# Layer 2 keys: statistics a batch ahead, a second key buffer, half-row token layout, the bound of the scores a batch late

## The chip, the cores and the metric

The kernel runs on one core of one Trainium2 chip. The metric is the device time in microseconds (us) of one execution, start to end; the median of three timed runs before the change is 7727.34 us (7716.75 to 7728.98). Beside the timed runs there is one profiled execution, from which every trace number here is read.

## The reference

The reference is a four-layer network on an image batch `x` of shape (8, 56, 56, 128), float32. Layer 0 is a deformable convolution block, layer 1 whitens the result (64 rows, five Newton-Schulz steps), layers 2 and 3 are attention followed by a mixture of 64 experts. Only the attention of layer 2 matters here. Each image becomes S = 3136 tokens of 128 channels (56 x 56, row by row), and the attention works on normalised tokens:

```python
def _ln_t(v, eps=1e-5):
    m = jnp.mean(v, axis=-1, keepdims=True)
    s = jnp.var(v, axis=-1, keepdims=True)
    return (v - m) / jnp.sqrt(s + eps)

# layer 2 attention, HEADS = 8, D_K = 16
kqv = x @ W_k.T
h = kqv.reshape(B, S, HEADS, D_K).transpose(0, 2, 1, 3)
scores = jnp.einsum('bhqd,bhkd->bhqk', h, h) / jnp.sqrt(jnp.float32(D_K))
attn = jax.nn.softmax(scores, axis=-1)
ctx = jnp.einsum('bhqk,bhkd->bhqd', attn, h)

# how it is used
t = t + _L2_attn_ref(_ln_t(t), L2_attn_W_k, L2_attn_W_q, L2_attn_W_v, L2_attn_W_o)
```

Queries, keys and values are the same projection `h`. So the kernel needs, for each of the 8 images, the normalised tokens, the keys with channels on partitions (`kT`), the values with tokens on partitions (`va`), and one number for all images: a bound on the scores, from the largest squared length of a head's vector, which lets the softmax do without a maximum per row.

## The kernel before, in words

The kernel runs the layers one after the other: `conv_layer`, `whiten_layer` (which leaves its result `y` in device memory as [56 rows, 8 images, 56 columns, 128 channels]), and `token_layers`. The last begins with a few transposed weights, calls `attention_keys` once, and then `attend`, the long part of the kernel, which reads the keys and values back from device memory.

`attention_keys` loops over the 8 images ("batches", `n`). For one batch it does this, in the order of the program:

1. Load the tokens into `t_sb`, a tile of 112 partitions by 28 tokens by 128 channels (lines 1060 to 1062), in two transfers of 56 partitions: partition `h * 56 + w` holds the tokens of column `w` in the image rows of parity `h`. In device memory each run is one token, 512 bytes. Line 1063 stores the same tile to `tok`, the token list that the later stage reads, also 512 bytes a run. The tile `t` has two buffers.
2. Statistics, lines 1066 to 1068: 28 pairs of `bn_stats` and `bn_aggr` on VectorE (DVE).
3. `rsqrt` (lines 1136 to 1142): DVE adds the epsilon (line 1140), GpSimd (POOL) raises to the power -0.5 (line 1141). The result `rs` has 112 x 28 elements.
4. Seven groups of four token columns: DVE normalises each 112 x 128 piece (`normalize`, line 112) into `xn` (two buffers), TensorE (PE) transposes it (line 121), ScalarE (ACT) copies the group out of PSUM into a 448-wide piece of `xT` (line 122), the normalised tokens with channels on partitions. `xT` has two buffers.
5. Keys: for two groups of heads, seven matmuls of 448 columns (line 1083), moved out of PSUM alternately by DVE (line 1091, even) and ACT (line 1087, odd) into `kT`, which has one buffer. Each half is then stored (line 1094).
6. Values: 25 matmuls of up to 128 tokens (line 1098), moved out alternately by DVE (line 1108) and ACT (line 1106) into `va`, one of two standing buffers, then stored in two transfers (line 1110).
7. The bound: POOL squares all values (line 1117), DVE sums each head's 16 squares (line 1119, 128 x 3200 elements in) and takes the largest (line 1120) into column `n` of `tops`.

After the loop a short chain turns `tops` into `low` and the flag `small`, on which the branch to `attend` waits. All PSUM tiles of the stage share six buffers (tag `m`).

All token, key and value transfers are issued by SyncE (SP) on one queue, in order: an instruction of that queue that waits holds up those behind it. The order of the instructions on each engine is not that of the program. A planner runs through the program with costs of its own and lets each engine take the earliest instruction of the program that is ready by these costs; so work of the next batch can be placed into gaps of the present one, and a transfer ahead of others. The order is fixed when the kernel is built; on the chip each engine goes through its list and waits where an input is late. `advance` (line 438), used by the change, steps the first generator of a list to its next `yield` and drops it when it is done; it fixes only where in the program the instructions stand.

Of the kernel before, what the change touches and what calls it, by code (L numbers as in the profile page):

```python
# [8 lines left out]
F32 = mybir.dt.float32  # L9
# [3 lines left out]
ALU = mybir.AluOpType  # L13
AX = mybir.AxisListType
# [3 lines left out]
NB, IH, IW, C = 8, 56, 56, 128  # L18
S = IH * IW
T = 112  # L20
NT = S // T
GT = 4
NG = NT // GT
QC = GT * T
KT = -(-S // 128)
# [19 lines left out]
HD, DK = 8, 16  # L45
# [71 lines left out]
def transpose_group(nc, k, ps, tag, dst, src, copy):  # L117

    p = ps.tile([128, GT, T], F32, tag=tag, name="p_tr")
    for i in range(GT):  # L120
        nc.tensor.transpose(p[:, i, :], src[:, i, :], k.ident[:T, :T])  # L121
    copy(dst, p.rearrange("p a b -> p (a b)"))  # L122
# [315 lines left out]
def advance(gens, n=1):  # L438

    for g in list(gens[:n]):  # L440
        try:
            next(g)
        except StopIteration:
            gens.remove(g)
# [591 lines left out]
    return [(t, min(128, S - 128 * t)) for t in range(KT)]  # L1036


def attention_keys(tc, k, w, yv, tok, kT_out, va_out, low, small):

    nc = tc.nc
    n_b = yv.shape[1]
    with ExitStack() as ctx:
        cp = ctx.enter_context(tc.tile_pool(name="akc", bufs=1))
        bp = ctx.enter_context(tc.tile_pool(name="akb", bufs=2))
        ps = ctx.enter_context(tc.tile_pool(name="akp", bufs=6, space=PSUM))
        vas = []  # L1050
        for i in range(2):
            va = cp.tile([128, 2, KT, 4, 32], F32, name=f"va{i}")
            nc.gpsimd.memset(va, 0.0)
            nc.gpsimd.memset(va[:, :, : KT - 1, :, DK : DK + 1], 1.0)
            nc.gpsimd.memset(va[: S - 128 * (KT - 1), :, KT - 1, :, DK : DK + 1], 1.0)
            vas.append(va)
        tops = cp.tile([128, n_b], F32, name="tops")
        wk = w.wk.rearrange("p h d -> p (h d)")
        for n in range(n_b):
            t_sb = bp.tile([T, NT, C], F32, name="t")  # L1060
            for h in range(2):
                nc.sync.dma_start(t_sb[h * IW : (h + 1) * IW], yv[h, n])
            nc.sync.dma_start(tok[n].rearrange("(t p) c -> p t c", p=T), t_sb)
            mv = bp.tile([T, NT, 2], F32, name="mv")
            st = bp.tile([T, NT, 6], F32, name="st")
            for i in range(NT):
                nc.vector.bn_stats(st[:, i], t_sb[:, i])
                nc.vector.bn_aggr(mv[:, i], st[:, i])
            rs = rsqrt(nc, k, bp, mv, NT)
            xT = bp.tile([C, S], F32, name="xT")  # L1070
            for g in range(NG):
                xn = bp.tile([T, GT, C], F32, name="xn")
                for i in range(GT):
                    normalize(nc, xn[:, i], t_sb[:, g * GT + i], mv, rs, g * GT + i)
                transpose_group(
                    nc, k, ps, "m", xT[:, g * QC : (g + 1) * QC], xn, nc.scalar.copy
                )
            kT = bp.tile([128, 2, S], F32, name="kT", bufs=1)
            for g in range(2):
                for c in range(NG):  # L1080
                    cols = slice(c * QC, (c + 1) * QC)
                    p = ps.tile([128, QC], F32, tag="m", name="p_h")
                    nc.tensor.matmul(
                        p, wk[:, g * 128 : (g + 1) * 128], xT[:, cols], start=True, stop=True
                    )
                    if c % 2:
                        nc.scalar.activation(
                            kT[:, g, cols], p, AF.Identity, bias=w.one16, scale=DK**-0.25
                        )
                    else:  # L1090
                        nc.vector.tensor_scalar(
                            kT[:, g, cols], p, DK**-0.25, w.one16, ALU.mult, ALU.add
                        )
                nc.sync.dma_start(kT_out[n, g], kT[:, g])
            va = vas[n % 2]
            for t, m in key_tiles():
                p = ps.tile([128, 2, 4, DK], F32, tag="m", name="p_v")
                nc.tensor.matmul(
                    p[:m].rearrange("p g j d -> p (g j d)"),
                    xT[:, t * 128 : t * 128 + m],  # L1100
                    w.wv,
                    start=True,
                    stop=True,
                )
                if t % 2:
                    nc.scalar.copy(va[:m, :, t, :, :DK], p[:m])
                else:
                    nc.vector.tensor_copy(va[:m, :, t, :, :DK], p[:m])
            for g in range(2):
                nc.sync.dma_start(va_out[n, g], va[:, g].rearrange("p t j d -> p (t j d)"))  # L1110

            sq = bp.tile([128, 2 * KT * 4, DK], F32, name="sq", bufs=1)
            v = va.rearrange("p g t j d -> p (g t j) d")[:, :, :DK]
            nc.gpsimd.tensor_tensor(sq, v, v, ALU.mult)
            top = bp.tile([128, 2 * KT * 4], F32, name="top")
            nc.vector.tensor_reduce(top, sq, AX.X, ALU.add)
            nc.vector.tensor_reduce(tops[:, n : n + 1], top, AX.X, ALU.max)  # L1120

        col = cp.tile([128, 1], F32, name="top_c")
        nc.vector.tensor_reduce(col, tops, AX.X, ALU.max)
        p = ps.tile([1, 128], F32, tag="m", name="p_tc")
        nc.tensor.transpose(p, col, k.ident)
        one = cp.tile([1, 1], F32, name="top_1")
        nc.vector.tensor_reduce(one, p, AX.X, ALU.max)
        p = ps.tile([128, 1], F32, tag="m", name="p_low")
        nc.tensor.matmul(p, k.ones, one, start=True, stop=True)
        nc.vector.tensor_scalar(low, p, -(DK**-0.5), None, ALU.mult)  # L1130
        nc.vector.tensor_scalar(small, low[:1], -SMALL, None, ALU.is_ge)
        nc.vector.tensor_scalar(low, low, 1.0, None, ALU.subtract)
        nc.vector.tensor_tensor(low, low, w.one16, ALU.mult)


def rsqrt(nc, k, pool, mv, n):

    m = mv.shape[0]
    rs = pool.tile([m, n], F32, name="rs")
    nc.vector.tensor_scalar(rs, mv[:, :, 1], EPS, None, ALU.add)  # L1140
    nc.gpsimd.tensor_tensor(rs, rs, k.mhalf[:m, :n], ALU.pow)  # L1141
    return rs
# [1037 lines left out]
def token_layers(tc, k, a, y, out):  # L2180

    nc = tc.nc
    n_b = out.shape[0]
    with ExitStack() as ctx:
# [6 lines left out]
        kT_d = dp.tile([n_b, 2, 128, S], F32, name="kT_d")  # L2191
# [6 lines left out]
        with tc.tile_pool(name="tlr", bufs=1) as rp:  # L2198
# [33 lines left out]
            yv = y.rearrange("(t a) n w c -> a n w t c", a=2)  # L2232
            low = cp.tile([128, 1], F32, name="low")
            small = cp.tile([1, 1], I32, name="small")
            attention_keys(tc, k, w, yv, tok, kT_d, va_d, low, small)
        pooled = [cp.tile([C, n_b, E], F32, name=f"pooled{i}") for i in range(2)]
        low3 = cp.tile([128, 1], F32, name="low3")
        small3 = cp.tile([1, 1], I32, name="small3")
# [105 lines left out]
```

## Time and profile before

| what | value |
|---|---|
| median of three timed runs | 7727.34 us (7716.75, 7727.34, 7728.98) |
| the profiled execution: time and span | 7718.14 us, 7716.3 us |
| share of the span busy: PE, DVE, ACT, POOL | 84%, 68%, 54%, 38% |
| key stage: first token load issued, last values stored to `va` | 1589.5 us, 1933.0 us |
| DVE per batch: 28 normalisations; 28 statistics pairs; 8 key evictions; 13 value copies; the two reductions | 7.3; 7.3; 8 x 0.68; 13 x 0.29; 3.5 + 0.3 us |
| ACT per batch: 7 `xT` copies; 6 key evictions; 12 value copies | 7 x 0.53; 6 x 0.63; 12 x 0.27 us |
| POOL per batch: power; squares | 4.8; 5.5 us |
| bytes per batch: tokens in, tokens out, keys, values | 1.61, 1.61, 3.21, 3.28 MB |
| token packets: size | 512 bytes (51,378 of the stage's 55,491 packets are of 512 bytes to 2 KB) |

The stage takes about 344 us, 4% to 5% of the span. How to read the views: a line of the timeline has the start, the time taken, engine, source line, operation, output and inputs by their names in the program and the shapes; in square brackets the idle time in front of it and what ended that. Similar neighbours are merged. In the view of waits, "A <- B" is how long A's engine stood before A and was released by B: total, times, longest. In the groups, the numbers behind the bar are total busy time and the mean of one in nanoseconds. The stretches give each engine's busy time with the instruction count in brackets. PE's float32 matmuls run as two passes, each its own entry (an 'x28' of key matmuls in the trace is 14 in the program).

### The profile page before, as it was taken

Reading aid. Unit: us, or ns where it says so; the run is one execution under the profiler, and the core shown is the slowest. Engines: PE = TensorE matmul, PEld = TensorE weight load, DVE = VectorE, ACT = ScalarE, POOL = GpSimd, SP = SyncE. Lnnn points to the kernel's source line nnn. Section 1 sums busy time; section 2 is a strip of 40 time slices with the busy share of each in tenths; the row PEclk is TensorE's granted clock in tenths of the full one; section 3 lists DMA queues with packets and bytes.
Section 4 is the critical chain, followed back from the end, with each engine's and each line's share of the span. In section 5 each row is a group of like instructions: output and inputs, shape, how many; then the busy total and the mean of one; then the engine's idle time right before and its main releaser. Section 6 shows DMA issues by size and latency. Waiting matters only on the chain. (4 is left out here: it accounts for less than half of the span.)

```text
span 7716.3 us, 157926 instructions
## 1 busy us (share of the span) xinstructions
PE 6482.3 (84%) x59883; PEld 2880.7 (37%) x59883; DVE 5284.8 (68%) x9856; ACT 4142.6 (54%) x6467; POOL 2935.1 (38%) x2555
## 2 busy tenths in 40 slices
PE   6659999556899999999999999999999997556654
PEld 4446666334233323323323323333333333245532
DVE  7975564366677777777777777777777776366752
ACT  4424444122666666666666666666666664056740
POOL 0011111022444444444444444444444443434653
PEclk8768898777999999999999999999999998788766
DMA  5453443376788778778778778778778775543543
GB/s 155 137 119 76 86 95 65 82 240 207 199 203 197 193 192 199 189 192 201 191 184 204 188 183 207 183 191 205 185 190 206 182 190 137 196 117 107 134 135 130
DMA packets 736303, 1287.38 MB, mean 167 GB/s; under 512 B 117698, under 2 KB 503108, under 8 KB 728516
## 3 DMA queue, kind: packets, MB, share of 16 engines
q1 hardware_dynamic: 725556, 1260.76, 65.1%
q0 software_dynamic: 6144, 12.60, 0.6%
q8 instruction: 484, 7.93, 0.5%
q10 hardware_dynamic: 3824, 3.68, 0.2%
q14 instruction: 295, 2.42, 0.1%
HBM read 286.04 MB, written 197.81 MB: 63 GB/s over the span
## 5 line engine op out<-in xcount | busy, mean ns | idle before, releaser
L1260 ACT ACTIVATE e<-p_s 128x768 f32<-128x768 f32 (+2 forms) x3712 | 2887.8, 830 | 1584.9 <-PE p_s L1252 1329.8
L1298 POOL COPY x<-sq 32x1152 f32<-32x1152 f32 x1792 | 2059.2, 1149 | 2067.6 <-PE p_s L1252 1330.0
L1271 DVE STREAM_TRANSPOSE sq<-e 128x768 f32<-128x768 f32 x2688 | 2434.5, 950 | 567.3 <-ACT e L1260 312.9
L1252 PE MATMUL p_s<-q,kT 32*128 32x384 f32 (+2 forms) x14848 | 1888.6, 548 | 33.6 <-ACT e L1260 18.6
L1305 PE MATMUL av<-e,va 128*32 128x384 f32 (+2 forms) x14848 | 1645.3, 515 | 30.4 <-DVE acc L1324 20.7
L1305 PE MATMUL avx<-x,va 128*32 128x384 f32 x10752 | 1138.3, 496 | 69.5 <-issue 40.2
L1252 PEld LDWEIGHTS p_s<-q,kT 32*128 32x128 f32 (+1 forms) x14848 | 654.8, 181 | 1252.6 <-issue 825.4
L1305 PEld LDWEIGHTS av<-e,va 128*32 128x32 f32 (+1 forms) x14848 | 294.5, 108 | 1049.4 <-issue 941.7
L1305 PEld LDWEIGHTS avx<-x,va 128*32 128x32 f32 x10752 | 353.2, 111 | 650.9 <-issue 595.2
L609 POOL TENSOR_TENSOR rs<-rs,mhalf 112x4 f32<-112x4 f32 x112 | 116.1, 1036 | 788.3 <-DVE rs L608 788.3
L1324 DVE TENSOR_TENSOR acc<-acc,avx 128x384 f32<-128x384 f32 x336 | 183.9, 547 | 229.9 <-PE avx L1305 228.6
L121 PE MATMUL p_tr<-ident,xn 112*128 112x112 f32 x672 | 134.6, 341 | 187.4 <-DVE xn L112 141.8
L1141 POOL TENSOR_TENSOR rs<-rs,mhalf 112x4 f32<-112x4 f32 (+2 forms) x136 | 168.1, 1236 | 269.3 <-DVE ntop L1942 123.8
L525 ACT COPY wT<-p_w 88x448 f32<-88x448 f32 x152 | 138.0, 922 | 194.1 <-PE p_w L523 161.4
L1990 ACT ACTIVATE xn<-t,ms,rs 112x128 f32<-112x128 f32 x448 | 185.3, 488 | 76.4 <-DVE ms L1983 76.4
L327 DVE SCALAR_TENSOR_TENSOR acc<-xp,dw,acc 128x3136 f32<-128x3136 f32 x56 | 194.3, 3478 | 31.3 <-ACT acc L322 31.2
L637 PE MATMUL p_f<-x1T,w 128*128 128x448 f32 x448 | 205.6, 583 | 4.4 <-DVE x1T L632 2.7
L121 PEld LDWEIGHTS p_tr<-ident,xn 112*128 112x128 f32 x672 | 98.7, 169 | 285.0 <-issue 185.1
L1385 POOL TENSOR_TENSOR rs<-rs,mhalf 128x3 f32<-128x3 f32 (+1 forms) x72 | 58.5, 815 | 365.0 <-DVE rs L1384 343.0
L523 PE MATMUL p_w<-ident,wide 112*88 112x112 f32 x896 | 146.5, 303 | 58.6 <-DMA px<-strips 34.1
L621 DVE TENSOR_TENSOR y<-y,p_rs 128x448 f32<-128x448 f32 x112 | 69.3, 619 | 176.6 <-PE p_rs L614 176.6
L122 ACT COPY xT<-p_tr 128x448 f32<-128x448 f32 x112 | 59.6, 532 | 229.8 <-PE p_tr L121 203.7
(354 smaller groups left out, 7830.9 us busy)
## 6 DMA issues: line engine op xcount, KB each, us to landing
x<-sq SPq DMA_DIRECT2D x5376, 144.0 KB
w<-in_L_ffn_weight_dram SPq DMA_DIRECT2D x64, 1024.0 KB
px<-strips SPq DMA_DIRECT2D x64, 616.0 KB
va_d<-va SPq DMA_DIRECT2D x16, 1600.0 KB
xT_d<-xT SPq DMA_DIRECT2D x112, 224.0 KB
xT<-xT_d SPq DMA_DIRECT2D x112, 224.0 KB
kT_d<-kT SPq DMA_DIRECT2D x16, 1568.0 KB
t<-t_a SPq DMA_DIRECT2D x16, 1568.0 KB
```

What stands on the lines that cost most here:

```text
L121: nc.tensor.transpose(p[:, i, :], src[:, i, :], k.ident[:T, :T])
L327: nc.vector.scalar_tensor_tensor(acc, xp[:, j // 3 : j // 3 + IH, j % 3 : j % 3 + IW], dw[:, j : j + 1], acc, ALU.mult, ALU.add,)
L523: nc.tensor.transpose(p[:, g], around[:, :, g], k.ident[:T, :T])
L637: nc.tensor.matmul(p, q.w1[:, f * 128 : (f + 1) * 128], x1T, start=True, stop=True)
L1141: nc.gpsimd.tensor_tensor(rs, rs, k.mhalf[:m, :n], ALU.pow)
L1252: nc.tensor.matmul(ss[j // 2][:m, j % 2, :width], kT[rows, 128 * i : 128 * i + m], q[rows, :width], start=True, stop=True,)
L1260: nc.scalar.activation(e[:m, 2 * j : 2 * j + 2, :width], ss[j][:m, :, :width], AF.Exp)
L1271: nc.vector.transpose(sq[:, :, i, j : j + 2].rearrange("p s j c -> p j s c"), exps[u, b, a, i][:, j : j + 2, :QB].rearrange("p j (s c) -> ...
L1298: nc.gpsimd.tensor_copy(*moves.pop(0))
L1305: nc.tensor.matmul(out, keys[u, b][1][:m, i, j, :], e[j], start=start, stop=stop)
L1324: nc.vector.tensor_tensor(to, to, in_order(av), ALU.add)
L1990: nc.scalar.activation(out[:, i], x[:, i], AF.Identity, bias=ms[:, i : i + 1], scale=rs[:, i : i + 1])
```

## The change

The tokens are laid out differently: partition `f * 56 + h` now holds the 28 tokens of half `f` of image row `h`. A partition's tokens are one run of 14,336 bytes in `y` and in `tok`; load and store are two transfers of 56 partitions each. Since a transposed group of four now holds tokens that are 28 apart, PE's output is viewed as [channels, 4, 2, 56], and ACT's copy writes it to its places in `xT`, 56 elements in a row of steps of 56 elements (224 bytes); `xT` ends in token order as before, but each group writes columns all over it.

Loading, statistics and `rsqrt` become a generator, `statistics(n)`. That of batch 0 runs at the start. In batch `n` that of `n + 1` is started before the normalisation and stepped after each of the 14 key matmuls: the tokens' store and four statistics pairs in the first step, four pairs in each of the next six, `rsqrt` in the eighth. The bound becomes a generator, `largest(n)`: the squares stand where they stood, after batch `n`'s values, but the two reductions come after the normalisation of batch `n + 1`. `kT` gets the pool's two buffers. Arithmetic and the number of compute instructions are the same; there is one token store more per batch.

```diff
-        for n in range(n_b):
+        def statistics(n):
             t_sb = bp.tile([T, NT, C], F32, name="t")
-            for h in range(2):
-                nc.sync.dma_start(t_sb[h * IW : (h + 1) * IW], yv[h, n])
-            nc.sync.dma_start(tok[n].rearrange("(t p) c -> p t c", p=T), t_sb)
+            inner = tok[n].rearrange("(h f i) c -> f h i c", f=2, i=NT)
+            for f in range(2):
+                of = slice(f * IH, (f + 1) * IH)
+                nc.sync.dma_start(t_sb[of], y[:, n, f * NT : (f + 1) * NT])
+            yield
+            for f in range(2):
+                nc.sync.dma_start(inner[f], t_sb[f * IH : (f + 1) * IH])
             mv = bp.tile([T, NT, 2], F32, name="mv")
             st = bp.tile([T, NT, 6], F32, name="st")
             for i in range(NT):
                 nc.vector.bn_stats(st[:, i], t_sb[:, i])
                 nc.vector.bn_aggr(mv[:, i], st[:, i])
-            rs = rsqrt(nc, k, bp, mv, NT)
+                if i % GT == GT - 1:
+                    yield
+            stats[n] = t_sb, mv, rsqrt(nc, k, bp, mv, NT)
+
+        def largest(n):
+            sq = bp.tile([128, 2 * KT * 4, DK], F32, name="sq", bufs=1)
+            v = vas[n % 2].rearrange("p g t j d -> p (g t j) d")[:, :, :DK]
+            nc.gpsimd.tensor_tensor(sq, v, v, ALU.mult)
+            yield
+            top = bp.tile([128, 2 * KT * 4], F32, name="top")
+            nc.vector.tensor_reduce(top, sq, AX.X, ALU.add)
+            nc.vector.tensor_reduce(tops[:, n : n + 1], top, AX.X, ALU.max)
+
+        stats, tail = {}, []
+        ahead = [statistics(0)]
+        while ahead:
+            advance(ahead)
+        for n in range(n_b):
+            t_sb, mv, rs = stats.pop(n)
+            if n + 1 < n_b:
+                ahead.append(statistics(n + 1))
+                advance(ahead)
             xT = bp.tile([C, S], F32, name="xT")
+            by_place = xT.rearrange("c (h f i) -> c i f h", f=2, i=NT)
             for g in range(NG):
...
-                transpose_group(
-                    nc, k, ps, "m", xT[:, g * QC : (g + 1) * QC], xn, nc.scalar.copy
-                )
-            kT = bp.tile([128, 2, S], F32, name="kT", bufs=1)
+                p = ps.tile([C, GT, 2, IH], F32, tag="m", name="p_tr")
+                for i in range(GT):
+                    nc.tensor.transpose(
+                        p[:, i].rearrange("c f h -> c (f h)"), xn[:, i], k.ident[:T, :T]
+                    )
+                nc.scalar.copy(by_place[:, g * GT : (g + 1) * GT], p)
+            advance(tail)
+            kT = bp.tile([128, 2, S], F32, name="kT")
             for g in range(2):
                 for c in range(NG):
...
                         p, wk[:, g * 128 : (g + 1) * 128], xT[:, cols], start=True, stop=True
                     )
+                    advance(ahead)
...
-            sq = bp.tile([128, 2 * KT * 4, DK], F32, name="sq", bufs=1)
-            v = va.rearrange("p g t j d -> p (g t j) d")[:, :, :DK]
-            nc.gpsimd.tensor_tensor(sq, v, v, ALU.mult)
-            top = bp.tile([128, 2 * KT * 4], F32, name="top")
-            nc.vector.tensor_reduce(top, sq, AX.X, ALU.add)
-            nc.vector.tensor_reduce(tops[:, n : n + 1], top, AX.X, ALU.max)
+            tail.append(largest(n))
+            advance(tail)
+        while tail:
+            advance(tail)
```

The caller passes `y` itself instead of its view by row parity.

More of the change, by code (lines that the diff above doesn't have):

```diff
@@ L1036, in key_tiles, with attention_keys @@
     return [(t, min(128, S - 128 * t)) for t in range(KT)]
-def attention_keys(tc, k, w, yv, tok, kT_out, va_out, low, small):
+def attention_keys(tc, k, w, y, tok, kT_out, va_out, low, small):
     nc = tc.nc
-    n_b = yv.shape[1]
+    n_b = y.shape[1]
     with ExitStack() as ctx:
@@ L1094, in attention_keys @@
                 nc.sync.dma_start(kT_out[n, g], kT[:, g])
+            assert not ahead
             va = vas[n % 2]
@@ L2234, in token_layers @@
             small = cp.tile([1, 1], I32, name="small")
[L2235 removed]
+            attention_keys(tc, k, w, y, tok, kT_d, va_d, low, small)
         pooled = [cp.tile([C, n_b, E], F32, name=f"pooled{i}") for i in range(2)]
```

## The prediction

> **What bounds the kernel now.** I read the page, then the stretches, the waits, the groups and the timeline of the one stage the change touches. The chain of work that ended last is no help: it covers the last 1% and lies in another stage. The key stage runs from the first token load (SP, 1589.5 us) to the last value tile (1933.0 us). One batch, by stretches (us, busy time of PE, weight loads, DVE, ACT, POOL, then granted clock, DMA share, GB/s):
>
> ```profile
> 1691.28:1734.60 43.32, 24.84 (x106) 16.56 (x106) 27.37 (x109) 10.72 (x25) 10.31 (x2) 0.70 0.71 225
> ```
>
> No engine fills it: PE works 24.8 of 43.3 us, DVE 27.4. So order of work sets the time, as that batch's timeline shows (start, us, what):
>
> ```profile
> 1681.66 3.49 DVE L1119 TENSOR_REDUCE top<-sq 128x200 f32<-128x3200 f32 x1 [2.75 <-POOL sq L1117]
> ...
> 1686.45 4.79 POOL L1141 TENSOR_TENSOR rs<-rs,mhalf 112x28 f32<-112x28 f32 x1 [4.82 <-DVE rs L1140]
> 1691.28 7.28 DVE L112 TENSOR_SCALAR xn<-t,mv,rs 112x128 f32<-112x128 f32 x28 [4.91 <-POOL rs L1141]
> ...
> 1691.78 6.58 PE L121 MATMUL p_tr<-ident,xn 112*128 112x112 f32 x25 [16.16 <-DVE xn L112]
> ...
> 1700.23 10.67 PE L1083 MATMUL p_h<-xT,wk 128*128 128x448 f32 x26
> ...
> 1710.73 5.88 PE L1098 MATMUL p_v<-wkT,xT 128*128 128x128 f32 x50
> ...
> 1717.10 5.52 POOL L1117 TENSOR_TENSOR sq<-va 128x3200 f32<-128x3200 f32 x1 [25.86 <-DVE va L1108]
> ```
>
> After one batch's values come the squares on POOL (5.5 us), their reduction on DVE (3.5), the last statistics, the power on POOL (4.8), and only then the next batch is normalised; PE stands still for 16.2 us. Over the stage (total us, times, longest):
>
> ```profile
> POOL sq L1117 <- DVE va L1108: 205.1, 8, 26.6
> ...
> PE p_tr L121 <- DVE xn L112: 141.8, 8, 28.6
> ...
> DVE xn L112 <- POOL rs L1141: 32.4, 8, 5.0
> ```
>
> The first normalisations, right after each power, begin at 1614.6, 1650.0, 1691.3, 1734.5, 1786.8, 1823.1, 1864.9 and 1908.3: a mean period of (1908.3-1614.6)/7 = 42.0 us. Most statistics of batch n+1 already lie between the evictions of batch n, so it is the tail (reduction, power) that is late, and in some batches the load: the 52.3 us period has tokens landing at 1774.3.
>
> **What the Trainium skill says.** (1) "SBUF — State Buffer", section "Who interferes with whom": a tensor_scalar in SBUF can take the port pair that DVE shares with GpSimd; the pair is an exclusive lock, and tensor_reduce never takes it. The trace agrees. The first line below is a 0.18 us instruction that stood behind the squares (POOL, 1639.51 to 1645.03); the second is four normalisations that at 0.26 us a step should take 1.1 us and took 2.1, behind a POOL addition (7435.47, 1.26 us):
>
> ```profile
> 1640.08 4.99 DVE L1140 TENSOR_SCALAR rs<-mv 112x28 f32<-112x28 f32 x1
> ...
> 7435.51 2.08 DVE L112 TENSOR_SCALAR chosen<-chosen,cmv,rs 128x128 f32<-128x128 f32 x4
> ```
>
> (2) "DMA: Bandwidth & Descriptors", "Specifications", gives 512 bytes as the least for line rate. The trace disagrees: with only 512-byte token runs in flight it moved 181 GB/s (1596 to 1602) and 168 (1650 to 1653) at full DMA share; rows of 12 KB of keys and values moved 410 (1641 to 1647) and 419 (1677 to 1686). The measurement decides. (3) The same page, "Why a DMA increments its semaphore by 16 and not by 1": a copy of 56 rows is spread over 14 engines (largest divisor up to 16). No run shows it; I take 14/16 of 410 = 359 GB/s. (4) "SBUF", "Specifications (TRN2)": leaving a 16-byte line at each element costs. It agrees with two copies of one shape, dense and strided (448 bytes a step), 532 against 926 ns:
>
> ```profile
> L122 ACT COPY xT<-p_tr 128x448 f32<-128x448 f32 x112 | 59.6, 532 | 229.8 <-PE p_tr L121 203.7 <-ACT xn L1990 17.6 <-issue 8.5
> ...
> L551 ACT COPY smp<-p_smp 128x448 f32<-128x448 f32 x56 | 51.9, 926 | 110.8 <-PE p_smp L544 110.4
> ```
>
> **The change, part by part.**
>
> *Half rows.* Loads and stores of tokens (1.61 MB each way a batch) go from 512 B to 14,336 B runs. At about 175 GB/s they take 18.4 us a batch, then 2 x 1.61/0.359 = 9.0. With 6.49 MB of keys and values at 0.41 (15.8 us) DMA needs 24.8 us a batch; before it was some 34 of 42. SP has the same four token, key and value issues plus one more store (0.4 us). The first load, issued at 1589.5, landed at 1601.9; now 4.5 us of transfer and about 2 us of latency (estimate: the time between the last bytes and later waits of this queue) give 1596. Gain 5.9 us. If 56 rows ran no faster than 512 B pieces, this is nothing.
>
> *Strided xT.* 56 copies grow from 532 to about 926 ns (steps of 224 bytes; the 112-byte copy on line 525 takes 922). A group of four normalisations takes 4 x 0.26 = 1.04 us, so ACT keeps pace and only the last group shows: +0.4 us a batch. But now every copy writes columns all over xT, so the first key matmul waits for the seventh copy: from the first normalisation 7.3 + 0.4 (PE) + 0.9 + 0.3 = 8.9 us, where it was 6.9. If a copy cost more than 1.04 us, each 0.1 us above adds 0.7 us a batch.
>
> *Statistics ahead.* The 28 pairs (28 x 0.26 = 7.3 us of DVE) and the power (4.8, POOL) move under batch n's key matmuls. The power leaves the path; POOL is idle there, so it costs nothing; without that cover it is 4.8 us a batch. Behind the statistics on DVE stand the key evictions, and behind those PE, which has six PSUM buffers of lead. The next tokens land in time: queued behind 3.28 MB of values they need 8.0 + 4.5 + 2 = 14.5 us from the batch's start, and DVE asks at 11 to 17.
>
> *Second kT.* The store of the old keys made others wait 0.6 us in all: nothing, either way.
>
> *Bound late.* The reduction (3.5 + 0.3) follows the next normalisation, so PE works beneath it. The squares still start when the values end, which is now when DVE wants to normalise. By (1) one blocks the other: a loss between 0 and 5.5 us a batch. I take 5.5, since DVE either stands in the normalisation or, if it keeps the ports, then at the reduction that waits for the squares.
>
> *Sum.* A middle batch on DVE from its first normalisation: 7.3 + 5.5 stall + 3.8 reductions = 16.6; statistics 7.3 and the four DVE evictions of the first key half 4 x 0.68 = 2.7, so 26.6; PE was held by PSUM and does its last two key tiles, 1.5, so 28.1; 25 value tiles at 0.235 (5.88/25) = 5.9; last copy 0.3. Together 34.3 us. The first batch has no stall: 8.9 + 14 x 0.75 + 6.2 = 25.6, say 26. The last has no statistics: 12.8 + 1.6 + 10.5 + 6.2 = 31. The first normalisation moves from 1614.6 to 1608.7. End of values: 1608.7 + 26 + 6 x 34.3 + 31 = 1871.5 instead of 1933.0. Gain 61.5 us. What follows (last squares, bound, attention) does the same as before. The span of 7716.3 becomes 7654.8, the profiled run of 7718.1 becomes 7656.6. The timed runs were 7716.8, 7727.3 and 7729.0; with the profiled one their mean is 7722.8, and 7722.8 - 61.5 = 7661 is my number.
>
> **Rivals.**
>
> *A, 0.50:* as summed, 7661; its own range is 7645 to 7680.
>
> *B, 0.25: no stall.* The code is put in order by a planner that filled DVE gaps with other batches' work before; it may put statistics or some normalisations under the squares or before them. Then 7.3 + 3.8 + 10 + 1.5 + 5.9 + 0.3 = 28.8 a batch: 6 x 5.5 + 5.5 = 38.5 more, 7622. For it: bn_stats has one SBUF input and ran under the squares at 0.25 us. Against: rs was planned beneath the squares and stood.
>
> *C, 0.15: the order stays.* If the planner believes the tokens late, statistics fall behind the values again and the power stays on the path. Only the transfers gain: 5.9 at the start and about 3 us a period (a mean of 39, the undisturbed ones being 35.4 and 41.3), 7 x 3 + 5.9 = 27, 7696. For it: in batches 4 and 7 they fell there. Against: that was after late loads, now halved.
>
> *D, 0.05: slower, by the strided copy.* If the 224-byte step with 56 in a row costs far more than both strided copies measured, ACT sets the transposes' pace: the gain is gone when 56 x (c - 1.04) = 61.5, c = 2.1 us, and 0.2% is lost from 2.4 us. Both known strides stand at 0.92 to 0.93, so this is remote; at 2.6 us it gives 7748.
>
> The remaining 0.05 is no difference that can be told, by two small failures together.
>
> **How the numbers follow.** About 0.2%, 15 us, is what a measurement of this kernel can tell from no change. A, B and C are faster by more: 0.90; same 0.05; slower 0.05. The range takes in B's and C's times with a few us for the runs' spread: 7614 to 7698.
>
> **What would show it.** Right: powers begin during the key matmuls; PE's wait for xn falls from 141.8 to about 60 us; one normalisation or reduction of 4 to 5.5 us per batch beside the squares; xT copies near 0.92 us; token landings 6 to 7 us after an idle queue; periods near 34. Wrong: xT copies above 1.1 us; powers still after the squares; DVE waiting for t in every batch; tokens under 200 GB/s; or another stage changing by more than 10 us.

## The result, and the profile after

The change makes the kernel slower. The median is 7774.03 us (7767.39 to 7781.31, four runs) against 7725.65 (7716.75 to 7728.98) before: a ratio of 1.0065, 95% interval 1.0047 to 1.0082, where the prediction had 7661. The profiled spans are 7773.5 and 7716.3 us. The key stage carries nearly all of it: from the first normalisation to the last squares on POOL it took 1610.8 to 1978.0 = 367.2 us after, and 1614.6 to 1933.2 = 318.6 before: 48.6 us more. The spans differ by 57.2 us; 12.4 of these lie behind the stage, where the program is unchanged, and the first normalisation comes 3.8 us earlier.

The stretches of the changed kernel first, one batch from normalisation to normalisation (columns as in the prediction: PE, weight loads, DVE, ACT, POOL, then clock, DMA share, GB/s):

```profile
1699.50:1750.24 50.74, 26.78 (x106) 17.23 (x106) 27.70 (x108) 13.93 (x25) 10.32 (x2) 0.67 0.55 193
```

PE has the 106 matmuls and DVE the work that they had in the 43.3 us of before. PE is busy 1.9 us longer, at a lower clock (0.67 against 0.70), and ACT 3.2 us, by the strided copies; what grew most is the time in which PE stands still. The timeline of the next batch shows where:

```profile
1728.35 5.52 POOL L1087 TENSOR_TENSOR sq<-va 128x3200 f32<-128x3200 f32 x1 [28.87 <-DVE va L1147]
...
1733.90 3.49 DVE L1090 TENSOR_REDUCE top<-sq 128x200 f32<-128x3200 f32 x1 [5.72 <-POOL sq L1087]
1737.42 0.36 DVE L1091 TENSOR_REDUCE tops<-top 128x1 f32<-128x200 f32 x1
1737.70 0.48 DVE L1075 BATCH_NORM_STATS2 st<-t 112x6 f32<-112x128 f32 x2
...
1745.41 4.80 POOL L1174 TENSOR_TENSOR rs<-rs,mhalf 112x28 f32<-112x28 f32 x1 [11.54 <-DVE rs L1173]
1750.24 7.27 DVE L112 TENSOR_SCALAR xn<-t,mv,rs 112x128 f32<-112x128 f32 x28 [4.91 <-POOL rs L1174]
1750.73 7.28 PE L1110 MATMUL p_tr<-ident,xn 112*128 112x112 f32 x28 [22.87 <-DVE xn L112]
...
1759.08 12.32 PE L1120 MATMUL p_h<-xT,wk 128*128 128x448 f32 x28 [1.07 <-ACT xT L1113]
1771.24 5.88 PE L1137 MATMUL p_v<-wkT,xT 128*128 128x128 f32 x50
1777.61 5.52 POOL L1087 TENSOR_TENSOR sq<-va 128x3200 f32<-128x3200 f32 x1 [27.41 <-DVE va L1147]
```

The statistics, which the change says are a batch ahead, stand behind the values, the squares and the reductions. The pause from the squares' start to the next normalisation, 1750.24 - 1728.35 = 21.9 us, is a chain: squares 5.5, reductions 3.9, 28 statistics pairs 7.5, `rs` and power 5.1. None lies under PE, and in that order the late bound is not late either. Six of the seven pauses are of this length. Before, pauses varied from 10.5 to 27.6 us, since most statistics lay between evictions in some batches; seven together were 113.6 us, now 128.6 (the first counts as -2.6, since its normalisation begins before the squares). The rest of the 48.6 us is the way from normalisation to squares: 25.6 us on average before, now 34.8 in batches 0 and 1 (in the first the statistics fall inside it, in the second the normalisation begins among the values and stands beside the squares), and 27.4 to 28.9 after that. Of these last 2.6 us or so, 1.9 are the wait for all seven strided copies, which was forecast.

The waits of the stage (total us, times, longest) answer those of before:

```profile
POOL sq L1087 <- DVE va L1147: 198.5, 8, 28.9
PE p_tr L1110 <- DVE xn L112: 162.0, 9, 22.9
...
DVE xn L112 <- POOL rs L1174: 34.4, 7, 5.0
```

PE's wait for `xn` grew from 141.8 to 162.0 us, where the prediction wanted about 60, and DVE still waits for the power in seven batches.

Were the tokens late? No. The statistics at 1737.70 are of batch 3, loaded from 1678.65 on. SP issued the store of its second half, which waits for that half, by 1692.81 + 3.75 = 1696.6 us: before batch 2 was normalised (1699.5), and 41 us before DVE came to them. DVE waited for tokens once in the stage, for the first ones (6.3 us).

Those first tokens show that another step failed. They were issued at 1587.39:

```profile
1594.08 4.30 SPq L1071 DMA_DIRECT2D tok<-t  x2
1598.22 0.49 DVE L1075 BATCH_NORM_STATS2 st<-t 112x6 f32<-112x128 f32 x2 [6.29 <-DMA t<-y]
```

The first half was there at 1594.1 (its store goes out), the whole only at 1598.2, 10.8 us after its issue; before, 12.4. Two stretches give the rate, with almost only token loads in flight:

```profile
1592.00:1594.00 2.00, 0.00 (x0) 0.00 (x0) 0.00 (x0) 0.00 (x0) 0.00 (x0) 0.50 0.88 208
1594.00:1596.00 2.00, 0.00 (x0) 0.00 (x0) 0.00 (x0) 0.00 (x0) 0.00 (x0) 0.50 0.92 194
```

The last column has 208 and 194 GB/s, where stretches of the same kind before (1594 to 1602) gave 162 to 190. Fourteen-kilobyte runs instead of 512 bytes brought some 12% to 14%, not the factor of two of the forecast.

### The profile page after: what moved, and what is told of

Its sections match the earlier page's. It is cut to its first block, busy times and chain, and to the rows that moved or that the text cites. A ratio compares the mean times of both kernels' runs of the same rounds, so it can differ in the third digit from the quotient of the medians.

```text
span 7773.5 us, 157967 instructions
## 1 busy us (share of the span) xinstructions
PE 6501.7 (84%) x59883; PEld 2881.6 (37%) x59883; DVE 5276.2 (68%) x9856; ACT 4170.2 (54%) x6467; POOL 2942.6 (38%) x2555
## 5 line engine op out<-in xcount | busy, mean ns | idle before, releaser
L1338 PE MATMUL av<-e,va 128*32 128x384 f32 (+2 forms) x14848 | 1646.5, 515 | 30.4 <-DVE acc L1357 20.7
L523 PE MATMUL p_w<-ident,wide 112*88 112x112 f32 x896 | 145.6, 302 | 58.7 <-DMA px<-strips 34.1
L1110 PE MATMUL p_tr<-ident,xn 112*128 112x112 f32 x224 | 58.0, 432 | 162.0 <-DVE xn L112 162.0
L642 PE MATMUL p_f<-hid,w 128*128 128x448 f32 x448 | 180.4, 545 | 0.8 <-issue 0.8
L288 PE MATMUL p_in<-w_in,xp 128*113 128x128 f32 x448 | 95.3, 383 | 94.2 <-DVE pj L295 73.6
```

The lines of the kernel that those rows point to most:

```text
L523: nc.tensor.transpose(p[:, g], around[:, :, g], k.ident[:T, :T])
L642: nc.tensor.matmul(p[:, :QC], q.w2[:, f], hid[:, f], start=(f == 0), stop=(f == 3))
L1338: nc.tensor.matmul(out, keys[u, b][1][:m, i, j, :], e[j], start=start, stop=stop)
```

## The experiments

Ratios are to runs of the kernel before on the same chip, with 95% intervals. A "period" is the time from one batch to the next in the profiled execution; a table of the whole stage in each kernel stands at the end of this section.

**1. The same change in the order of the program.** All five engines follow the written order in this stage; nothing else is changed.

```diff
+        ctx.enter_context(
+            tc.manual_schedule(
+                engines={
+                    e.engine for e in (nc.tensor, nc.scalar, nc.vector, nc.gpsimd, nc.sync)
+                }
+            )
+        )
         stats, tail = {}, []
```

> The changed kernel with the key stage issued in the order of the program on every engine, instead of the planner's. Theory 1 (the planner's order is the loss: it puts all 28 statistics pairs of the next batch behind the values and the reduction of the present one, though the tokens landed some 40 us earlier): powers during the key matmuls, periods near 34 us, 7668 us with a few us either way. Theory 2 (the layout itself is the loss: strided xT copies near 1.0 us, the first key matmul behind all seven copies, normalisation blocked by the squares): no faster than before, 7725 us or more.

Measured: 7729.33 us, ratio 1.0003 (0.9993 to 1.0013). That is the time of the second theory, though not by its mechanism: experiment 7 puts the old layout into the same order and finds no difference. The loss goes with the planner's order, but the written order did not bring the gain that I had forecast for it: the period is 42.6 us, not 34.3. The timeline of this kernel shows two terms of that (the pairs below are consecutive):

```profile
1698.06 12.52 DVE L112 TENSOR_SCALAR xn<-t,mv,rs 112x128 f32<-112x128 f32 x28
1698.31 5.53 POOL L1087 TENSOR_TENSOR sq<-va 128x3200 f32<-128x3200 f32 x1 [5.12 <-DVE va L1154]
...
1716.85 0.29 DVE L1075 BATCH_NORM_STATS2 st<-t 112x6 f32<-112x128 f32 x1 [2.48 <-DMA t<-y]
...
1717.28 0.26 DVE L1075 BATCH_NORM_STATS2 st<-t 112x6 f32<-112x128 f32 x1
1717.57 0.18 DVE L1076 BATCH_NORM_AGGREGATE mv<-st 112x2 f32<-112x6 f32 x1
1717.67 0.26 DVE L1075 BATCH_NORM_STATS2 st<-t 112x6 f32<-112x128 f32 x1
```

The normalisations stand 12.52 - 7.27 = 5.2 us beside the squares, as forecast (5.5). But a pair takes 0.39 us (1717.28 to 1717.67), not 0.26: the aggregation directly behind its own statistics waits for them. 28 pairs cost 3.7 us more. And the tokens come 2.5 us late, 18.8 us after the batch's start where the forecast had 14.5. The planner interleaves the pairs of neighbouring tokens, which is where I had read 0.26.

**2. Pairs skewed by one.** The kernel of experiment 1, with each aggregation one place later:

```diff
                 nc.vector.bn_stats(st[:, i], t_sb[:, i])
-                nc.vector.bn_aggr(mv[:, i], st[:, i])
+                if i:
+                    nc.vector.bn_aggr(mv[:, i - 1], st[:, i - 1])
...
+            nc.vector.bn_aggr(mv[:, NT - 1], st[:, NT - 1])
             stats[n] = t_sb, mv, rsqrt(nc, k, bp, mv, NT)
```

> The kernel in program order, with each bn_aggr issued one place later, behind the next bn_stats, as the planner had it. In program order a pair took 0.395 us, because the second of a pair waits for the first; in the planner's order 0.26. Theory 1 (the sum missed this and other small terms; each can be taken away): 28 x 0.135 = 3.8 us less per period, periods near 39 us, 7700 us, within 12 us. Theory 2 (PE sets the period by its half clock after each pause, DVE's time is hidden): no change from the kernel in program order, 7720 to 7735 us.

Measured: 7696.43 us, ratio 0.9958 (0.9941 to 0.9975), period 37.5, and the timeline has a pair every 0.26 us again:

```profile
1709.59 0.26 DVE L1075 BATCH_NORM_STATS2 st<-t 112x6 f32<-112x128 f32 x1
1709.77 0.17 DVE L1077 BATCH_NORM_AGGREGATE mv<-st 112x2 f32<-112x6 f32 x1
1709.85 0.26 DVE L1075 BATCH_NORM_STATS2 st<-t 112x6 f32<-112x128 f32 x1
```

So the change in a written order with skewed pairs gains 0.4%. From this kernel its parts can be taken back one at a time.

**3. The bound at its old place.** One step more of `largest(n)` directly behind the squares:

```diff
             tail.append(largest(n))
             advance(tail)
+            advance(tail)
```

> Against the kernel in program order with skewed pairs (7696.4), this one differs in one thing: the two reductions of batch n follow its squares at once, ahead of the normalisation of batch n+1, as they stood before the change. T1 (the late bound gains what lies beneath the squares and the reductions, less the stall of the normalisation): on DVE the wait for the squares, 5.7 us, and the reductions, 3.9, come onto the path and the stall of 5.2 goes: +4.4 us a batch, seven times 31, so 7727 +- 10, slower than with the bound late by 0.4%. T2 (the late bound is worth nothing, since the stall eats it): 7696 +- 8, normalisations at 7.3 us and the period still near 37.5.

Measured: 7729.04 us, ratio 1.0006 (0.9999 to 1.0013), period 40.95. The late bound is worth 0.48% by the ratios and 33 us between the two medians; the stage itself is 24 us shorter with it in the traces, seven periods of 3.4 us. So it gains in spite of its stall (31 expected).

**4. The statistics behind the reductions.** The kernel of experiment 3, and in addition the statistics and the power where the planner had put them (the store of the tokens moves with them, behind the value stores):

```diff
                         p, wk[:, g * 128 : (g + 1) * 128], xT[:, cols], start=True, stop=True
                     )
-                    advance(ahead)
...
             tail.append(largest(n))
             advance(tail)
+            advance(tail)
+            while ahead:
+                advance(ahead)
```

> The same as the kernel with the bound early, but the 28 statistics pairs and the power of batch n+1 also stand behind the reductions of batch n, which is the order that the planner gave the changed kernel, here written by hand with skewed pairs. T1 (this place alone makes the change slower): a pause of about 22 us between values and normalisation, a period near 50 us, which is 12.5 more than with the statistics among the keys (37.5): 7696 + 7 x 12.5 = 7783 +- 15, at least as slow as the changed kernel (7774). T2 (something else in the planner's order is to blame, transfers or other engines): the statistics behind the values cost at most the power and half of the pairs, under 9 us a batch, 7750 or less.

Measured: 7776.96 us, ratio 1.0074 (1.0056 to 1.0093): the time of the changed kernel. Its timeline has the same pause, 1767.51 - 1745.62 = 21.9 us, and a period near 50 us:

```profile
1745.62 5.52 POOL L1089 TENSOR_TENSOR sq<-va 128x3200 f32<-128x3200 f32 x1 [27.26 <-DVE va L1154]
1751.17 3.48 DVE L1092 TENSOR_REDUCE top<-sq 128x200 f32<-128x3200 f32 x1 [5.72 <-POOL sq L1089]
...
1762.68 4.79 POOL L1184 TENSOR_TENSOR rs<-rs,mhalf 112x28 f32<-112x28 f32 x1 [11.54 <-DVE rs L1183]
1767.51 7.28 DVE L112 TENSOR_SCALAR xn<-t,mv,rs 112x128 f32<-112x128 f32 x28 [4.91 <-POOL rs L1184]
```

The place of the statistics and the power costs 0.68%, some 50 us (48 between the medians, 62 of the stage in the traces, where all seven pauses have this length and not six), and reproduces the result: the cause is shown from the written side.

**5. One key buffer.** The kernel of experiment 2 with `kT` at one buffer:

```diff
-            kT = bp.tile([128, 2, S], F32, name="kT")
+            kT = bp.tile([128, 2, S], F32, name="kT", bufs=1)
```

> The kernel in program order with skewed pairs (7696.4), with one buffer of keys in place of two. T1 (the second buffer brings nothing, as forecast): 7696 +- 8, and DVE and ACT wait for no store of keys. T2 (with the shorter period the stores of keys come late, and the buffer is now needed): waits of the first key evictions of 2 us or more a batch, 7710 or more.

Measured: 7693.36 us, ratio 0.9967 (0.9954 to 0.9981). The second buffer does nothing, as forecast.

**6. The half rows alone, and the change without them, in the planner's order.** First the kernel before with the new token layout only, then the changed kernel with the old layout only. The core of both edits:

```diff
-            for h in range(2):
-                nc.sync.dma_start(t_sb[h * IW : (h + 1) * IW], yv[h, n])
-            nc.sync.dma_start(tok[n].rearrange("(t p) c -> p t c", p=T), t_sb)
+            for f in range(2):
+                of = slice(f * IH, (f + 1) * IH)
+                nc.sync.dma_start(t_sb[of], y[:, n, f * NT : (f + 1) * NT])
+            for f in range(2):
+                nc.sync.dma_start(inner[f], t_sb[f * IH : (f + 1) * IH])
...
-                transpose_group(
-                    nc, k, ps, "m", xT[:, g * QC : (g + 1) * QC], xn, nc.scalar.copy
-                )
...
+                nc.scalar.copy(by_place[:, g * GT : (g + 1) * GT], p)
```

(for the second kernel the lines with minus are put back and those with plus taken out).

> The kernel before with the half-row token layout alone; planner's order. Its planned order hides the statistics of every second batch and puts those of the others behind the values. Theory 1: periods alternate, near 37 and near 50 us, mean 43.5; first tokens 6 us earlier; 7725 to 7738 us. Theory 2 (layout): all periods some 4 to 8 us longer than before's, 7755 to 7790 us, most of the change's loss.

> The changed kernel without the half-row layout (tokens by parity of the row, 512-byte runs, dense xT copies); the other three parts stay; planner's order. From the fourth batch on all statistics lie behind the values, ahead of the reduction. Theory 1: the order alone costs about what the change costs, less the 7.4 us of statistics that run beside the squares: periods near 42 us, 7715 to 7740 us. Theory 2 (layout): without the layout the rest of the change gains, 7700 us or less.

Measured: half rows alone 7752.57 us, ratio 1.0039 (1.0027 to 1.0051), between what the theories asked; the change without them 7716.02, 0.9989 (0.9982 to 0.9996), at the lower end of what the first theory asked. Taken out of the changed kernel, the half rows give back 58 us. Why, the built order of DVE shows (N normalisation, K key eviction, v value copy, T and t the two reductions, s statistics, R `rs`; one of the later batches, which repeat):

```
changed kernel:          N28 K8 v13 T t s28 R
without half rows:       N28 K8 v13 s28 T t R
half rows alone:         N28 K8 v13 T t s28 R  and  N28 K5 s4 KsssKs4 Kv4 svvsvsvsvvsvsvsvs10 R T N t,  in turn
```

With the old layout the planner put the statistics behind the values too, but under the squares. With half rows it put them behind the reductions: in every second batch of the kernel with half rows alone, whose periods alternate between 38 to 40 and 54 to 55 us, and in every batch but the first of the changed kernel.

**7. The half rows in a fixed order.** Experiment 1 with the old layout (the same lines again):

> The kernel in program order without the half-row layout: tells the layout's own effect under one fixed order of work. Theory 1 (the layout costs about 1.5 us a batch by strided copies and the wait for the seventh, and saves 4.7 us a batch of token transfer that DVE waits for here, and 6 us at the start): slower than the kernel in program order by some 28 us, 7745 to 7770 us. Theory 2 (the layout itself is the loss): faster than it, 7715 us or less.

Measured: 7730.55 us, ratio 1.0007 (0.9996 to 1.0018), as experiment 1; neither theory had this. In one fixed order the layout does nothing that can be told: DVE waits for tokens 20.7 us in the stage with half rows and 32.4 without; what takes that back, I put down to the strided copies without having tried it. So the 58 us are the planner's order, not the transfers.

**8. Less on SP's queue, in the planner's order.** Two kernels leave the changed kernel as it is and let ACT issue one kind of transfer, the token loads in one, the value stores in the other:

```diff
-                nc.sync.dma_start(t_sb[of], y[:, n, f * NT : (f + 1) * NT])
+                nc.scalar.dma_start(t_sb[of], y[:, n, f * NT : (f + 1) * NT])
```

```diff
-                nc.sync.dma_start(va_out[n, g], va[:, g].rearrange("p t j d -> p (t j d)"))
+                nc.scalar.dma_start(va_out[n, g], va[:, g].rearrange("p t j d -> p (t j d)"))
```

> The changed kernel with the token loads issued by ACT instead of SP, so that they don't stand behind the stores in SP's order; planner's order, which now places the statistics among the key evictions. Theory 1: power off the path in every batch, 7650 to 7690 us. Theory 2: 7740 us or more as the layout is the same.

> The changed kernel in the planner's order, but the two stores of values are issued by ACT instead of SP; nothing else differs, and the tokens are loaded by SP as in the changed kernel. T1 (the planner put the statistics late only because its own account of SP's queue had the tokens late): the statistics now stand among the key evictions of every batch in the built order, powers begin during the key matmuls, period 36 to 42, 7690 to 7725. T2 (the statistics are late for a reason on the chip, and the issue from another engine helped otherwise): 7755 or more, with pauses of about 22 us.

Measured: token loads from ACT 7704.58 us, ratio 0.9974 (0.996 to 0.9988), half of the expected gain; value stores from ACT 7675.11, 0.9942 (0.9924 to 0.9961), more than expected. In both the built order has statistics among the keys; in the second a batch reads `N24 T t K s12 K s8 K s8 K K R K K K v7 NvvNvNvNvv`. Its timeline:

```profile
1718.63 11.49 DVE L112 TENSOR_SCALAR xn<-t,mv,rs 112x128 f32<-112x128 f32 x24
1730.05 3.47 DVE L1090 TENSOR_REDUCE top<-sq 128x200 f32<-128x3200 f32 x1
...
1744.27 4.79 POOL L1174 TENSOR_TENSOR rs<-rs,mhalf 112x28 f32<-112x28 f32 x1 [19.86 <-DVE rs L1173]
1753.41 5.53 POOL L1087 TENSOR_TENSOR sq<-va 128x3200 f32<-128x3200 f32 x1 [4.34 <-DVE va L1147]
```

This is nearly the order that the prediction had summed: normalisation with its stall (11.49 - 24 x 0.26 = 5.3 us), reductions, statistics among the keys, the power under them; but four of the 28 normalisations already stand among the values of the batch before. The middle period is (1855.04 - 1650.60)/6 = 34.1 us; the forecast had 34.3. In the first kernel the planner left 20 normalisations beside the squares (10.40 us) and put eight of the next batch right behind `rs`, so that DVE stands 4.91 us for the power in the middle of the keys, and PE behind it for DVE's next key eviction (4.6 us): a gain half spent.

**9. Tokens earlier, then the squares on ACT.** To the kernel of experiment 2: first, the tokens of batch n+2 are loaded ahead of the value stores of batch n; then also the squares by ACT, behind the next batch's `xT` copies, with the reductions after the first half of the keys.

```diff
-        def statistics(n):
+        tokens = {}
+        def load(n):
+            tokens[n] = bp.tile([T, NT, C], F32, name="t")
...
+            if n + 2 < n_b:
+                load(n + 2)
             va = vas[n % 2]
```

```diff
-            nc.gpsimd.tensor_tensor(sq, v, v, ALU.mult)
+            nc.scalar.activation(sq, v, AF.Square)
...
-            advance(tail)
             kT = bp.tile([128, 2, S], F32, name="kT")
...
                 nc.sync.dma_start(kT_out[n, g], kT[:, g])
+                if g == 0:
+                    advance(tail)
```

> As the one before, with the tokens two batches ahead asked for before the values are stored, so that they don't queue behind 3.28 MB of values and half the keys. Theory 1: DVE's wait for tokens, 2.5 us in each period, goes: periods near 36.5 us, 7684 us, within 12 us. Theory 2: no further change.

> As the one before, with the squares on ACT behind the xT copies of the next batch instead of on POOL, and the reductions after the first half of the keys. Theory 1 (the squares on POOL block the normalisation on DVE for 5.2 us a period): no normalisation stands, periods near 31 us, 7646 us, within 15 us. Theory 2 (the block is hidden by PE's pace): 7675 us or more.

Measured: early load 7690.45 us, ratio 0.9958 (0.994 to 0.9976). DVE's waits for tokens fall from 20.0 to 6.6 us, but the period stays at 37.4 and the ratio is that of experiment 2: a gain isn't shown. Squares on ACT as well: 7642.02 us, ratio 0.9883 (0.9861 to 0.9904), period 30.6. A line each from its timeline, its groups and its stretches:

```profile
1682.86 7.25 DVE L112 TENSOR_SCALAR xn<-t,mv,rs 112x128 f32<-112x128 f32 x28
```

```profile
L1091 ACT ACTIVATE sq<-va 128x3200 f32<-128x3200 f32 x8 | 23.0, 2880 | 0.5 <-DVE va L1163 0.5
```

```profile
1676.01:1706.67 30.66, 27.48 (x106) 16.66 (x106) 26.52 (x109) 16.76 (x27) 4.80 (x2) 0.83 0.88 301
```

The normalisations run at full pace, the stall is gone, and PE works 27.5 of 30.7 us. Engine and place of the squares changed together, and the reductions moved too; squares on POOL at that later place were not tried. This version beats both kernels: 84 us less than before, by the medians, and 132 less than the changed one, which was timed in another set of runs.

**The stage in every kernel.** From the first normalisation to the last value copy in the profiled execution, and how far stage and median lie from the kernel before (us; medians against those of the kernel before on the same chip):

| kernel | stage | stage, difference | median, difference |
|---|---|---|---|
| before | 318.4 | | |
| the change | 367.0 | +48.6 | +48.4 |
| 1, written order | 320.9 | +2.5 | +2.8 |
| 2, skewed pairs | 292.1 | -26.3 | -29.8 |
| 3, bound early | 316.4 | -2.0 | +5.6 |
| 4, statistics last | 378.0 | +59.6 | +53.5 |
| 5, one key buffer | 289.1 | -29.3 | -30.1 |
| 6, half rows alone | 346.9 | +28.5 | +26.0 |
| 6, change without half rows | 308.9 | -9.5 | -10.5 |
| 7, written order, old layout | 324.9 | +6.5 | +4.3 |
| 8, token loads from ACT | 299.0 | -19.4 | -22.0 |
| 8, value stores from ACT | 271.6 | -46.8 | -48.3 |
| 9, early load | 287.9 | -30.5 | -35.8 |
| 9, squares on ACT | 242.0 | -76.4 | -84.2 |

The two columns agree within 8 us. What follows the last value copy is the same program in all of them and took 5767.6 to 5795.6 us in these executions, so a single span by itself can't settle a difference of that size; the stage can.

## Why the prediction was wrong

**What bounds the kernel** held: order sets the time of this stage, and the later gains came by shortening the pause.

**Statistics ahead** is the step that failed. I read the order of the program as the order on the chip. The sum moved 7.3 us of statistics and 4.8 of power off the path in every batch; the planner, not the program, decided, and it put both onto the path in six of seven pauses. Experiment 4 sets the cost of that place at some 50 us; experiment 8 shows that the same program gains when one kind of transfer leaves SP's queue, which changes the planner's order. That the planner held the tokens for late is the reading that fits: on the chip they lay there 41 us before their turn. Its own account of the queue appears in no trace, so this last link is argued.

**Rival C** named this place and expected a smaller gain, 7696. It erred twice. It counted only gains from faster transfers; but before, all 28 pairs stood behind the reduction in one batch of seven (the pause of 27.6 us; the prediction named two), and in the others most lay between evictions or under the squares. Behind the reductions they lose that cover: 7.5 us in nearly every batch. And it was held unlikely because "that was after late loads, now halved": the planner's account counts, not the load on the chip, and the loads were not halved. The case that ended slower, the strided copy, was the wrong mechanism for that side.

**Half rows**: 359 GB/s forecast, 194 to 208 measured; landing after 6.5 us forecast, 10.8 measured; gain from issue to first normalisation 5.9 us forecast, 1.7 measured (25.1 to 23.4). I took the 512-byte pieces for the cause of the low rate, and the 410 GB/s for what longer runs would bring; but those 410 were stores that reach all 128 partitions. The Trainium skill, "SBUF — State Buffer", section "Door 1: The DMA port swizzle (why `[64,N]` ≈ `[32,N]`)", which I didn't draw on, says that the ports reached by a transfer's partitions set its rate, and gives 196 GB/s for 64 partitions of a 1 MiB transfer and 328 for all 128. A token transfer has 56 partitions in both kernels. Three other stretches of the trace of before, each with one kind of transfer in flight, part the two readings: loads of layer 1 (line 888: 64 partitions, rows of 14,336 bytes), loads of keys and values by `attend` (lines 1222 and 1224: 128 partitions, rows of 2,048 bytes or less), and stores of layer 1 (line 1003: 64 partitions, rows of 14,336 bytes):

```profile
1448.00:1476.00 28.00, 3.77 (x25) 3.03 (x25) 1.14 (x8) 0.00 (x0) 0.00 (x0) 0.50 1.01 213
1957.00:1961.00 4.00, 2.20 (x10) 1.29 (x12) 0.00 (x0) 0.19 (x1) 0.00 (x0) 0.50 1.06 384
1560.00:1565.00 5.00, 5.00 (x13) 2.15 (x12) 2.03 (x3) 1.75 (x3) 0.00 (x0) 1.00 1.00 384
```

For loads the trace agrees with the page: long rows on 64 partitions move 213 GB/s, short rows on all partitions 384. For stores it doesn't: 64 partitions at a time, the two halves in turn, moved 384. The 12% to 14% between the two token layouts is what was left for the size of the pieces. No run loaded tokens on all partitions, so for the token load itself the cause is argued, not shown. The prediction's conclusion that the trace disagrees with 512 bytes as the least for line rate doesn't follow either: it compared loads to 56 partitions with stores from 128.

**Strided copies**: 995 ns against a forecast of 926, still under the 1.04 us of four normalisations, so they cost what was said. The first key matmul came 1759.08 - 1750.24 = 8.8 us after the first normalisation (8.9 forecast). The group, against 532 ns before:

```profile
L1113 ACT COPY xT<-p_tr 128x448 f32<-128x448 f32 x56 | 55.5, 995 | 189.7 <-PE p_tr L1110 150.9 <-DMA t<-y 37.6
```

**Second kT**: nothing, right (experiment 5). **Bound late**: the stall was right, 5.2 to 5.3 us, in experiments 1 and 8 and once in the changed kernel; and the part is worth 0.48% in a fixed order (experiment 3). In the changed kernel it could not act, since the next normalisation now stood behind the statistics, and these behind the reductions.

**The sum** met its middle term in experiment 8: 34.1 us a batch, forecast 34.3. That kernel gained 0.58%, 45 us, of the 61.5. Most of the missing part is in the first batch: from its first normalisation to its squares 34.9 us instead of 26, since the planner put all 28 pairs as one block between two key evictions, with PE waiting behind; another 4.2 us are the gain of the first load that didn't come (1.7 for 5.9 in the changed kernel). But the 34.1 is in part luck. Experiment 9's early load has the summed order to the letter, with pairs at 0.26 us and tokens in time, and its period is 37.4. One of its batches begins its normalisation at 1759.14; DVE is through with the statistics 26.0 us later (26.6 in the sum), PE begins the values after 29.1 (28.1), and they take until 1796.7:

```profile
1788.22 0.71 PE L1151 MATMUL p_v<-wkT,xT 128*128 128x128 f32 x4
...
1789.33 0.71 PE L1151 MATMUL p_v<-wkT,xT 128*128 128x128 f32 x4 [0.40 <-ACT va L1159]
```

That is 8.4 us where the sum had 5.9 + 0.3: the first seven tiles wait for their copies on ACT. That in experiment 8 the four normalisations among the values made up for this is what the two orders suggest; it was not tried by itself. In the written order of experiment 1 the sum missed two more: pairs at 0.39 us when not interleaved, and tokens at 18.8 instead of 14.5 us. The chances lay on one side as well: 0.90 for a gain, and no case in which the planner's order makes the kernel slower.

## What to carry to other kernels

Where a planner orders the instructions, moving lines of the program is a request, not an edit: look at the built order of the busiest engine first, and price what happens if the moved work loses the cover that it has now. Before giving a load longer pieces, ask how many partitions it reaches. And a stall of one engine beside another can be worth as much as the order: the last step's 48 us came with the squares taken away from beside the normalisations, to another engine and a later place.

## What the runs showed of the hardware

- Two dependent small instructions on DVE, statistics and their aggregation, cost 0.39 us a pair back to back and 0.26 with another pair's instruction between them: over 8 x 28 pairs, and with what hangs on them, 29 us of the stage and 33 between the medians (experiments 1 and 2).
- The squares of 128 x 3200 float32 take 5.52 us on POOL and 2.88 on ACT. Beside the squares on POOL 28 normalisations take 12.5 us instead of 7.3; beside those on ACT DVE's statistics pairs keep their 0.26 us and a key eviction its 0.65 (1692.8 to 1694.3 in experiment 9). A normalisation beside ACT's squares was not tried.
- Loads to 64 partitions in 14,336-byte rows moved 213 GB/s, loads to 128 partitions in rows of at most 2,048 bytes 384, and stores from 64 partitions in 14,336-byte rows 384 as well (trace of the kernel before).
- Transposes do not hold PE's granted clock. After each pause of the changed kernel it is 0.50, and the 7.3 us of transposes do not bring it back, though PE is nearly always busy in them: in one batch they began at 1750.73, and the stretch 1761 to 1762 still has 0.50, the next 0.90. In the last kernel of experiment 9, where PE goes over from values to transposes with some 0.7 us of idle time, the clock falls in the midst of them: 1.00 in the stretch 1684 to 1685, 0.50 from 1686 on, and 1.00 again from 1696. The Trainium skill, "TensorE: Matmul & The Clock Gate", section "What's actually happening", gives about 3.4 us of sustained activity to full clock, seen through a free-running window. Counted from the first key matmul the clock came back after 1.2 to 4.4 us before and 2.9 to 5.9 in the changed kernel, so the traces fit no fixed time from there; which work counts as activity was not tried.
